# Queuing GpSimd's fetches, gathers, normalising and bias additions behind a slot's probability multiplies

## The chip, the cores and the metric

The kernel is one program on one core of a Trainium2 chip. The metric is the device time of one execution in microseconds; lower is better. Five engines work side by side, each through its own queue of instructions in order: TensorE (PE in the profile, with its weight loads as PEld), VectorE (DVE), ScalarE (ACT), GpSimd (POOL) and SyncE (SP). In this kernel GpSimd does arithmetic and also issues the DMAs that fetch rows by index, so that an issue and an addition stand in one line.

## The reference, cut to what matters

The input is 16 batches of 224 tokens of width 512, and for each batch a context of 750 rows of width 384 with a mask of the keys that count. The layer is a gated cross attention, then a gated feed-forward block whose two weights are rounded to -1, 0 or 1 and whose activations are rounded to 8 bits.

```python
q = layernorm(x) @ W_q                    # 8 heads of 64
k, v = context @ W_k, context @ W_v
sim = where(mask, q k^T / 8, -max)        # per batch and head
out = softmax(sim) v
x = x + tanh(g_xattn) * (out @ W_o + b_o)
h = bitlinear(layernorm(x), w1, b1)       # rmsnorm, 8-bit rows, ternary weights; 512 -> 2048
h = gelu(h)
x = x + tanh(g_ffn) * bitlinear(h, w2, b2)   # 2048 -> 512
```

## The kernel before, in words

**Slots.** The batches are sorted by how many keys their mask keeps, and each is worked on in a "slot" with a fixed room for keys: 192 in slots 0 to 7, 128 in slots 8 to 13, 64 in slots 14 and 15. Only the kept context rows are gathered. Token rows are taken in pairs of 128-row tiles: `x_i` (three buffers) is a pair to be normalised for the queries, and `y_i` (three buffers) the same rows again as the residual for what follows. There are 14 pairs. The gathered context `ctx_s` has two buffers.

**Attention of slot s.** The 8 heads and 224 queries are cut into four units n = 0 to 3. `scores` multiplies queries by keys on TensorE (`sim`, L1106), takes the masked logits and their maximum on DVE (L1120), the exponentials and their sums on ACT (L1130), the reciprocal `rec` of the sums on DVE (L1139), and multiplies the probabilities `p_s_n` by it on GpSimd (L1140). `turn_probs` transposes the probabilities on TensorE into `ptp` (L1163) and, where a slot has more than 128 keys, `ptr` (L1170); DVE or ACT copies them to `pT`, and `weighted` multiplies by the values (`av`, L1188). Units 0 and 1 of a slot are scored at the end of the slot before it, units 2 and 3 in the middle of the slot.

**Work for later slots, in the same loop pass.** For slot s+2: `norm(i)` takes statistics of a pair x_i on DVE and, on GpSimd, `rs_x`, `ls_x` (L1014, L1017), a power (L795) and the normalising itself (L1019, two instructions); `fetch` issues the next x pair (L808, two DMAs), and `gather` the context rows (L908, one or two DMAs). For slot s+1: the context is turned (`ctxp`, L935) and projected (`kp`, L946; `vp`, L962), and the queries are projected (`qp`, L1066). `select` builds the list of kept keys (`ind` on DVE, L846).

**The feed-forward block of pair i.** In slots 0 and 1 its weights are rounded and turned instead (`raw`, `w`, `wp`). From slot 2 on, `residual(i)` fetches y_i (L808, two DMAs) and adds the bias `bo` on GpSimd (L1245, two additions). `project(i, k)` multiplies by W_o on TensorE (`op`, L1252) and DVE adds the result to y (L1255). `normalise(i)` follows on DVE with its scale chain on GpSimd (L1307, L795, L1272 to L1274) and the bias `b2` (L1312). `up` is the first product (`hp`, L1333), `down` the second (`fp`, L1475), whose result DVE adds to y (L1488) and GpSimd stores (L1494). Slot 2 takes pair 0, slot 8 pair 6, slot 9 none, slot 10 pair 7, and slot 15 pair 12; pair 13 is done behind the loop. In a pass the order is `residual`, `up` of the pair before, `project`, `down`; in slots 2 and 10 there is no `up`.

**What sets the order.** In each pass three streams (attention, work for later slots, feed-forward) are merged by written costs; pieces with cost 0.0 come where they fall. A tile scheduler then orders every engine's queue from this program, from its own estimates of time and from when buffers come free; an engine works through its queue strictly in that order. `tc.issue_after(x)` says that what is issued inside it comes behind instruction x. The PSUM results of transposes and projections (`ptp`, `ptr`, `op`, `fp`, `vp`, `ctxp`) share four buffers of one pool, each of which comes free when the engine that reads it is done.

Of the kernel before, what the change touches and what calls it, by code (L numbers as in the profile page):

```python
# [11 lines left out]
ALU = mybir.AluOpType  # L12
# [722 lines left out]
def compact_path(ctx, tc, sh, x, context, out, late_loads, stages):  # L735
# [3 lines left out]
    nc = tc.nc  # L739
    P = 128  # L740
    B, S, D = x.shape
# [11 lines left out]
    NTOK = B * S // P  # L753
# [64 lines left out]
    live = [{} for _ in range(B + 1)]  # L818
# [9 lines left out]
    def home(s):  # L828

        return live[min(s, B - 2)], CAPS[s] if s == B - 1 else 0  # L830
# [162 lines left out]
    def fetch(i):  # L993
        if i:
            xp = pa.tile([P, 2, D], F32, tag="x", name=f"x_{i}", bufs=3)
        else:
            xp = early[:, : 2 * D].rearrange("p (k d) -> p k d", k=2)
        for k in range(2):
            fetch_x(xp[:, k, :], 2 * i + k)
        normed[i] = xp  # L1000

    def norm(i, ks=(0, 1)):

        xp = normed[i]
        name = f"x{i}_{ks[0]}"
        part = slice(ks[0], ks[-1] + 1)
        mv = small(f"mv_{name}", 4).rearrange("p (k n) -> p k n", k=2)
        for k in ks:
            st = small(f"bs_{name}_{k}", 6)
            nc.vector.bn_stats(st, xp[:, k, :])  # L1010
            nc.vector.bn_aggr(mv[:, k, :], st)
            load["v"] += 850
        rstd = small(f"rs_{name}")
        nc.gpsimd.tensor_scalar(rstd[:, part], mv[:, part, 1], 1.0, EPS, ALU.mult, ALU.add)  # L1014
        pow_half(rstd[:, part])
        less = small(f"ls_{name}")
        nc.gpsimd.tensor_scalar(less[:, part], mv[:, part, 0], -1.0, 0.0, ALU.mult, ALU.add)  # L1017
        for k in ks:
            nc.gpsimd.tensor_scalar(  # L1019
                xp[:, k, :], xp[:, k, :], less[:, k : k + 1], rstd[:, k : k + 1], ALU.add, ALU.mult  # L1020
            )
# [57 lines left out]
    def tiles_of(s):  # L1079

        return range(-(-s * S // P), -(-(s + 1) * S // P))

    def norm_pieces(s):
        pieces = []
        for t in tiles_of(s):
            if t % 2 == 0:
                pieces.append((0.0, lambda t=t: norm(t // 2)))
                if t // 2 + 2 < NTOK // 2:
                    pieces.append((0.0, lambda t=t: fetch(t // 2 + 2)))
        return pieces  # L1090


    UNITS = [(q, u) for u in range(2) for q in range(NQ)]
# [1 line left out]
    def scores(s, n):  # L1095
        st = live[s]
        keys, first = home(s)
        cap = CAPS[s]
        q, u = UNITS[n]
        sim = wide([TQ, 2, 2, 256], F32, f"sim_{s}_{n}")  # L1100

        begin = P if cap > P else 0
        for i in range(2):
            p = 2 * u + i
            for j in range(2):
                nc.tensor.matmul(  # L1106
                    sim[:, j, i, :cap],
                    lhsT=st["qT"][j * DH : (j + 1) * DH, p, q * TQ : (q + 1) * TQ],
                    rhs=keys["kT"][j * DH : (j + 1) * DH, p, first + j * begin : first + j * begin + cap],
                    start=True,  # L1110
                    stop=True,
                )
        probs = pa.tile([TQ, 4, 192], F32, tag="p", name=f"p_{s}_{n}", bufs=3)
        total = small(f"sum_{s}_{n}", 4)
        for i in range(2):
            for j in range(2):
                h = 2 * i + j
                nmax = pa.tile([TQ, 1], F32, tag="nm", name=f"nm_{s}_{n}_{h}", bufs=12)

                nc.vector.tensor_tensor_reduce(  # L1120
                    out=probs[:, h, :cap],
                    in0=sim[:, j, i, :cap],
                    in1=keys["mask"][:, first + j * begin : first + j * begin + cap],
                    scale=-(DH**-0.5),
                    scalar=FMAX,
                    op0=ALU.add,
                    op1=ALU.min,
                    accum_out=nmax,
                )
                nc.scalar.activation(  # L1130
                    probs[:, h, :cap],
                    probs[:, h, :cap],
                    AF.Exp,
                    bias=nmax,
                    scale=-1.0,
                    accum_out=total[:TQ, h : h + 1],
                )
        rec = small(f"rec_{s}_{n}", 4)
        nc.vector.reciprocal(rec[:TQ], total[:TQ])  # L1139
        nc.gpsimd.tensor_tensor(  # L1140
            probs[:, :, first : first + cap],
            probs[:, :, :cap],
            rec[:TQ].unsqueeze(2).to_broadcast([TQ, 4, cap]),
            ALU.mult,
        )
        load["v"] += 4 * (150 + 1.05 * cap + 83) + 150
        load["s"] += 4 * (250 + 0.96 * cap + 187)
        st["p", n] = probs
# [63 lines left out]
        for a in range(2):  # L1212
            evict(xoT[:, 2 * a : 2 * a + 2, at : at + S], by[:, a], 2 * S)

    def attention_pieces(s):
        a = 4.0 if CAPS[s] > P else 2.6
        t = 0.8 if CAPS[s] > P else 0.5
        c = 1.4 if CAPS[s] > P else 1.0

        def both(n):  # L1220
            scores(s, n)
            scores(s, n + 1)

        def wait():
            pass

        pieces = [(3.0, wait)]
        pieces += [(t, lambda n=n: turn_probs(s, n)) for n in (0, 1)]
        pieces += [(c, lambda: both(2)), (3.0, wait)]
        pieces += [(t, lambda n=n: turn_probs(s, n)) for n in (2, 3)]  # L1230
        pieces += [(1.0, wait), (a, lambda: weighted(s))]
        return pieces
# [2 lines left out]
    pairs = {}  # L1235
    late = {}

    def residual(i):

        f = pairs[i] = {}  # L1240
        f["y"] = y = late["rows"].tile([P, 2, D], F32, tag="y", name=f"y_{i}", bufs=3)
        for k in range(2):
            fetch_x(y[:, k, :], 2 * i + k)
        for k in range(2):
            nc.gpsimd.tensor_tensor(y[:, k, :], y[:, k, :], sh.bo, ALU.add)  # L1245

    def project(i, k):
        y = pairs[i]["y"]
# [446 lines left out]
    with ExitStack() as behind:  # L1695
        for instruction in latest.values():
            behind.enter_context(tc.issue_after(instruction))
        scores(0, 0)
        scores(0, 1)
        for _, piece in queries[3:] + keys_values[3:]:  # L1700
            piece()
        for c in range(NPC):
            sum_weights(0, c)
        scale_weights(0)
        for _, piece in norm_pieces(1):
            piece()
        select(2)

        held = [sh.wo[0:1, 0, 0:1], sh.wo[0:1, 2, 0:1], sh.wo[P // 2 : P // 2 + 1, 2, 0:1]]
        for dst in held + [sh.bo[0:1, 0:1], sh.b1[0:1, 0:1], sh.b2[0:1, 0:1]]:  # L1710
            nc.scalar.copy(dst, weight_sums[0][0:1, NPC - 1 : NPC])
    late_loads(True)

# [1 line left out]

    projected = raised = lowered = 0
    for s in range(B):
        other = norm_pieces(s + 2) if s + 2 < B else []
        if s + 2 < B:
            other.append((0.0, lambda s=s: gather(s + 2)))  # L1720
        if s + 3 < B:
            other.append((0.0, lambda s=s: select(s + 3)))
        if s + 1 < B:
            other += weave(context_pieces(s + 1), query_pieces(s + 1))
        flow = []
        if s < 2:
            flow = weight_pieces(s)
        else:
            complete = 256 * (projected + 1) <= S * s
            if projected == 0:  # L1730
                nc.gpsimd.tensor_scalar(sh.bo, sh.bo, sh.tgates[:, 0:1], None, ALU.mult)
                nc.gpsimd.tensor_scalar(sh.b2, sh.b2, sh.tgates[:, 1:2], None, ALU.mult)
            if complete:
                flow.append((0.0, lambda i=projected: residual(i)))
            if s == B - 1:
                flow += last_slot(projected)
            elif raised < projected:
                flow += up_pieces(raised)
                raised += 1
            if complete and s < B - 1:  # L1740
                flow += project_pieces(projected)
                projected += 1
                if lowered < raised:
                    flow += down_pieces(lowered)
                    lowered += 1
        merge(attention_pieces(s), other, flow)
        if s == 1:

            late["stage"].close()
            late["rows"] = ctx.enter_context(tc.tile_pool(name="rows", bufs=1))  # L1750
        if s + 1 < B:
            scores(s + 1, 0)
            scores(s + 1, 1)
# [17 lines left out]
        NTOK - 1: [(0, 128, where[2] + 96)],  # L1771
    }
    i = NPAIR - 1
    residual(i)
    with tc.issue_after(late["av"]), tc.issue_after(late["rounded"]):
        for k in range(2):
            for g in range(2):
# [10 lines left out]
    with tc.issue_after(late["rounded"]):  # L1788
        with tc.issue_after(lowered):
            projected = project(i, 0)  # L1790
# [3 lines left out]
    with tc.issue_after(normed):  # L1794
        with tc.issue_after(pairs[i - 1]["turned"]):
            projected = project(i, 1)
# [65 lines left out]
```

## Time and profile before

| | |
|---|---|
| runs | 723.97, 723.9 and 726.18 us; median 723.97 |
| profiled execution | span 726.0 us; of the three runs 726.18 is the one near it |
| busy TensorE, DVE, ACT, GpSimd | 674.0, 493.1, 413.0, 391.5 us |
| mean clock granted to TensorE | 0.986 of full |
| GpSimd's multiplies of probabilities (L1140) | 64 instructions, 78.6 us |

The span runs from the first to the last instruction. In the profile a row of a timeline has its start, its length, engine, line, operation, the tiles written and read with their shapes, and in brackets how long the engine was idle before and for what it waited. A row of TensorE's waits has the waiting instruction, what it waited for, the sum in microseconds, how often, and the longest.

### The profile page before, as it was taken

To read this page: it belongs to the slowest core of one execution; us is meant where nothing else is said; L and a number is where in the kernel's file an instruction comes from. 1 tells how busy PE (TensorE), PEld (TensorE's weight loads), DVE (VectorE), ACT (ScalarE), POOL (GpSimd) and SP (SyncE) were. 2 spreads that over 40 slices of the span, in tenths; PEclk is the share of its full clock that TensorE was granted. 3 is DMA by queue.
4 is the path that set the end of the run, shared out by engine and by line. 5 is a ranking of instruction groups with operands and counts; after the bars stand their busy time and mean duration, and the time that the engine had idled before them with its cause. 6 is when DMAs were issued, how large, how long until landed. Compare 5 with 4: busy or idle time off the path is not lost.

```text
span 726.0 us, 11445 instructions
## 1 busy us (share of the span) xinstructions
PE 674.0 (93%) x3917; PEld 430.3 (59%) x3917; DVE 493.1 (68%) x1296; ACT 413.0 (57%) x974; POOL 391.5 (54%) x545
## 2 busy tenths in 40 slices
PE   4996899999989999999798999999999999999984
PEld 3774686765656555656565566566666556554432
DVE  5495666777477476675575966757859393869993
ACT  2556664377484672674566646837556563656642
POOL 5584478553494444735646656457554535276441
PEclk9998999999999999999999999999999999999998
DMA  7784031022232122213232331312313222142211
GB/s 239 288 277 162 0 84 51 18 60 53 68 85 60 54 59 59 85 29 90 60 45 90 83 78 46 66 44 74 82 46 59 73 54 77 30 99 47 69 33 49
DMA packets 80146, 56.74 MB, mean 78 GB/s; under 512 B 68208, under 2 KB 68352, under 8 KB 79952
## 3 DMA queue, kind: packets, MB, share of 16 engines
q1 hardware_dynamic: 72336, 31.22, 18.1%
q0 software_dynamic: 7744, 24.71, 11.1%
q8 instruction: 33, 0.54, 0.3%
q14 instruction: 33, 0.27, 0.1%
HBM read 32.06 MB, written 7.34 MB: 54 GB/s over the span
## 4 chain that ended last, share of the span: by engine, by line
PE 56%; DVE 13%; issue 13%; POOL 10%; ACT 4%; DMA 2%; POOLq 0%; DVEq 0%
PE qp L1066 10%; PE op L1252 9%; PE hp L1333 8%; PE fp L1475 6%; PE kp L946 4%; PE sim L1106 4%; PE vp L962 4%; PE ptp L1163 3%; PE av L1188 2%; DVE a L1369 2%; POOL p L1140 2%; POOL out_dram L1494 1%; DVE hq L1372 1%; PE xnp L1045 1%; POOL y L1312 1%
## 5 line engine op out<-in xcount | busy, mean ns | idle before, releaser
L1140 POOL TENSOR_TENSOR p<-p,rec 112x768 f32<-112x768 f32 (+2 forms) x64 | 78.6, 1230 | 74.9 <-DVE rec L1139 28.8
L1130 ACT ACTIVATE p<-p,nm 112x192 f32<-112x192 f32 (+2 forms) x256 | 104.7, 412 | 9.9 <-DVE nm L1120 6.8
L1066 PE MATMUL qp<-xnT,wq_sb 128*128 128x224 f32 x512 | 105.3, 359 | 0.6 <-issue 0.6
L1252 PE MATMUL op<-wo_sb,xoT 128*128 128x512 f32 x224 | 104.0, 599 | 0.0
L1475 PE MATMUL fp<-w2T,hqT 128*128 128x512 fp8e4 x448 | 101.4, 379 | 2.4 <-ACT hqT L1355 1.3
L1333 PE MATMUL hp<-w1T,xqT 128*128 128x512 fp8e4 x416 | 99.7, 384 | 3.0 <-DVE nm L1120 1.3
L1066 PEld LDWEIGHTS qp<-xnT,wq_sb 128*128 128x128 f32 x512 | 97.1, 194 | 6.4 <-issue 4.1
L1341 DVE SCALAR_TENSOR_TENSOR h<-hp,c,b_bc 128x1024 f32<-128x1024 f32 x52 | 66.5, 1280 | 43.8 <-PE hp L1333 43.5
L1120 DVE CUSTOM_DVE_ANT_0 p<-sim,mask 112x192 f32<-112x192 f32 (+2 forms) x224 | 56.0, 303 | 31.9 <-PE sim L1106 31.5
L1475 PEld LDWEIGHTS <-hqT 128*128 128x128 bf16 x448 | 42.7, 98 | 56.3 <-issue 5.3
L1369 DVE TENSOR_REDUCE a<-h 128x1 f32<-128x2048 f32 x26 | 59.3, 2281 | 20.3 <-ACT h L1366 20.1
L1333 PEld LDWEIGHTS <-xqT 128*128 128x128 bf16 x416 | 40.0, 98 | 47.6 <-issue 8.9
L1252 PEld LDWEIGHTS op<-wo_sb,xoT 128*128 128x128 f32 x224 | 40.6, 190 | 38.3 <-issue 35.9
L1488 DVE SCALAR_TENSOR_TENSOR y<-fp,c,y 128x512 f32<-128x512 f32 x28 | 20.8, 745 | 62.1 <-PE fp L1475 59.3
L1494 POOL DMA_INDIRECT out_dram<-y,token x24 | 27.6, 1148 | 58.0 <-DVE y L1488 53.6
L946 PE MATMUL kp<-ctxT,wk_sb 128*128 128x192 f32 (+1 forms) x360 | 57.8, 308 | 0.0
L1382 ACT ACTIVATE h<-h 128x2048 f32<-128x2048 f32 x25 | 47.7, 1909 | 17.1 <-DVE hq L1372 11.8
L1312 POOL TENSOR_TENSOR y<-y,b_bc 128x512 f32<-128x512 f32 x28 | 37.0, 1322 | 37.2 <-DVE fx L1292 36.9
L781 ACT COPY pT<-ptp 128x448 f32<-128x448 f32 (+1 forms) x62 | 32.2, 535 | 42.2 <-PE ptp L1163 41.4
L946 PEld LDWEIGHTS kp<-ctxT,wk_sb 128*128 128x128 f32 x360 | 52.4, 193 | 5.5 <-issue 3.8
L1106 PE MATMUL sim<-kT,qT 64*112 64x192 f32 (+2 forms) x512 | 51.5, 314 | 1.8 <-issue 0.9
L781 ACT COPY qT<-qp 128x448 f32<-128x448 f32 x29 | 15.4, 532 | 65.9 <-PE qp L1066 60.3
(199 smaller groups left out, 1249.3 us busy)
## 6 DMA issues: line engine op xcount, KB each, us to landing
raw<-in_L_ffn_w_dram SPq DMA_DIRECT2D x16, 512.0 KB
wq_sb<-in_L_xattn_W_q_dram SPq DMA_DIRECT2D x1, 1024.0 KB
b_bc<-in_L_ffn_b_dram SPq DMA_DIRECT2D x1, 1024.0 KB
wk_sb<-in_L_xattn_W_k_dram SPq DMA_DIRECT2D x1, 768.0 KB
wv_sb<-in_L_xattn_W_v_dram SPq DMA_DIRECT2D x1, 768.0 KB
wo_sb<-in_L_xattn_W_o_dram SPq DMA_DIRECT2D x1, 512.0 KB
wo_sb<-in_L_xattn_W_o_dram SPq DMA_DIRECT2D x2, 256.0 KB
out_dram<-y SPq DMA_DIRECT2D x2, 256.0 KB
```

What stands on the lines that cost most here:

```text
L946: nc.tensor.matmul(pk[:, p - p0, :], lhsT=sh.wk[:, c, p * P : (p + 1) * P], rhs=st["ctxT"][:, c, :cap], start=(c == 0), stop=(c == NC - 1),)
L1066: nc.tensor.matmul(pq[:, i, :], lhsT=sh.wq[:, d, (p + i) * P : (p + i + 1) * P], rhs=st["xnT"][:, d, :], start=(d == 0), stop=(d == ND - 1),)
L1106: nc.tensor.matmul(sim[:, j, i, :cap], lhsT=st["qT"][j * DH : (j + 1) * DH, p, q * TQ : (q + 1) * TQ], rhs=keys["kT"][j * DH : (j + 1) * D ...
L1120: nc.vector.tensor_tensor_reduce(out=probs[:, h, :cap], in0=sim[:, j, i, :cap], in1=keys["mask"][:, first + j * begin : first + j * begin ...
L1130: nc.scalar.activation(probs[:, h, :cap], probs[:, h, :cap], AF.Exp, bias=nmax, scale=-1.0, accum_out=total[:TQ, h : h + 1],)
L1140: nc.gpsimd.tensor_tensor(probs[:, :, first : first + cap], probs[:, :, :cap], rec[:TQ].unsqueeze(2).to_broadcast([TQ, 4, cap]), ALU.mult,)
L1252: last = nc.tensor.matmul(po, lhsT=xoT[:, d, at : at + P], rhs=sh.wo[:, d, :], start=(d == 0), stop=(d == ND - 1))
L1333: last = nc.tensor.matmul(ph[:, n, :], lhsT=f["xqT"][:, k * ND + d, :], rhs=w1T[:, d, at : at + NB], start=(d == 0), stop=(d == ND - 1),)
L1341: nc.vector.scalar_tensor_tensor(h[:, cols], ph.rearrange("t i n -> t (i n)"), f["c1", k], sh.b1[:, cols], ALU.mult, ALU.add)
L1369: nc.vector.tensor_reduce(amax[:, k : k + 1], h, AX.X, ALU.max, apply_absolute_value=True)
L1382: nc.scalar.activation(f["h", k], f["h", k], AF.Square, accum_out=ss[:, k : k + 1])
L1475: last = nc.tensor.matmul(po, lhsT=f["hqT", k][:, n, :], rhs=w2T[:, n, :], start=(n == 0), stop=(n == NF - 1))
```

## The change

The pieces of work for later slots no longer fall where GpSimd's queue takes them. `scores` keeps the multiply of each unit as `scaled[s, n]`. From slot 2 on, the normalising, the fetch of x and the gather of a pass are issued behind the multiply of unit 1 of the slot; in slots 0 and 1 the fetch and the gather are issued behind unit 3, and the normalising stays as it was. In `residual` the two additions of `bo` go behind the multiply of unit 1 (for pair 13, behind unit 3 of slot 15); the fetches of y stay ahead. The fetch of an x pair is a piece of its own, emitted where the buffer comes free, behind the odd tile of a pair: three pairs ahead, where it was two pairs ahead at the normalising; `fetch(3)` moves to the prologue. No operation is added or taken away: all engines have as many instructions as before.

```diff
--- before.py
+++ after.py
@@ -1081,13 +1081,20 @@
         return range(-(-s * S // P), -(-(s + 1) * S // P))
 
     def norm_pieces(s):
-        pieces = []
-        for t in tiles_of(s):
-            if t % 2 == 0:
-                pieces.append((0.0, lambda t=t: norm(t // 2)))
-                if t // 2 + 2 < NTOK // 2:
-                    pieces.append((0.0, lambda t=t: fetch(t // 2 + 2)))
-        return pieces
+        return [(0.0, lambda t=t: norm(t // 2)) for t in tiles_of(s) if t % 2 == 0]
+
+    def fetch_pieces(s):
+
+        ahead = [t // 2 + 3 for t in tiles_of(s) if t % 2]
+        return [(0.0, lambda i=i: fetch(i)) for i in ahead if i < NTOK // 2]
+
+    def held(s, n, pieces):
+
+        def run(piece):
+            with tc.issue_after(live[s]["scaled", n]):
+                piece()
+
+        return [(c, lambda piece=piece: run(piece)) for c, piece in pieces]
 
 
     UNITS = [(q, u) for u in range(2) for q in range(NQ)]
@@ -1137,12 +1144,12 @@
                 )
         rec = small(f"rec_{s}_{n}", 4)
         nc.vector.reciprocal(rec[:TQ], total[:TQ])
-        nc.gpsimd.tensor_tensor(
+        st["scaled", n] = nc.gpsimd.tensor_tensor(
             probs[:, :, first : first + cap],
             probs[:, :, :cap],
             rec[:TQ].unsqueeze(2).to_broadcast([TQ, 4, cap]),
             ALU.mult,
-        )
+        ).ins
         load["v"] += 4 * (150 + 1.05 * cap + 83) + 150
         load["s"] += 4 * (250 + 0.96 * cap + 187)
         st["p", n] = probs
@@ -1212,7 +1219,7 @@
         for a in range(2):
             evict(xoT[:, 2 * a : 2 * a + 2, at : at + S], by[:, a], 2 * S)
 
-    def attention_pieces(s):
+    def attention_pieces(s, behind=()):
         a = 4.0 if CAPS[s] > P else 2.6
         t = 0.8 if CAPS[s] > P else 0.5
         c = 1.4 if CAPS[s] > P else 1.0
@@ -1226,7 +1233,7 @@
 
         pieces = [(3.0, wait)]
         pieces += [(t, lambda n=n: turn_probs(s, n)) for n in (0, 1)]
-        pieces += [(c, lambda: both(2)), (3.0, wait)]
+        pieces += [(c, lambda: both(2))] + list(behind) + [(3.0, wait)]
         pieces += [(t, lambda n=n: turn_probs(s, n)) for n in (2, 3)]
         pieces += [(1.0, wait), (a, lambda: weighted(s))]
         return pieces
@@ -1235,14 +1242,15 @@
     pairs = {}
     late = {}
 
-    def residual(i):
+    def residual(i, scaled):
 
         f = pairs[i] = {}
         f["y"] = y = late["rows"].tile([P, 2, D], F32, tag="y", name=f"y_{i}", bufs=3)
         for k in range(2):
             fetch_x(y[:, k, :], 2 * i + k)
-        for k in range(2):
-            nc.gpsimd.tensor_tensor(y[:, k, :], y[:, k, :], sh.bo, ALU.add)
+        with tc.issue_after(scaled):
+            for k in range(2):
+                nc.gpsimd.tensor_tensor(y[:, k, :], y[:, k, :], sh.bo, ALU.add)
 
     def project(i, k):
         y = pairs[i]["y"]
@@ -1704,10 +1712,11 @@
         scale_weights(0)
         for _, piece in norm_pieces(1):
             piece()
+        fetch(3)
         select(2)
 
-        held = [sh.wo[0:1, 0, 0:1], sh.wo[0:1, 2, 0:1], sh.wo[P // 2 : P // 2 + 1, 2, 0:1]]
-        for dst in held + [sh.bo[0:1, 0:1], sh.b1[0:1, 0:1], sh.b2[0:1, 0:1]]:
+        opened = [sh.wo[0:1, 0, 0:1], sh.wo[0:1, 2, 0:1], sh.wo[P // 2 : P // 2 + 1, 2, 0:1]]
+        for dst in opened + [sh.bo[0:1, 0:1], sh.b1[0:1, 0:1], sh.b2[0:1, 0:1]]:
             nc.scalar.copy(dst, weight_sums[0][0:1, NPC - 1 : NPC])
     late_loads(True)
 
@@ -1715,9 +1724,13 @@
 
     projected = raised = lowered = 0
     for s in range(B):
-        other = norm_pieces(s + 2) if s + 2 < B else []
+        other, loads = [], []
         if s + 2 < B:
-            other.append((0.0, lambda s=s: gather(s + 2)))
+            other = norm_pieces(s + 2)
+            loads = fetch_pieces(s + 1) + [(0.0, lambda s=s: gather(s + 2))]
+        if s > 1:
+
+            other, loads = held(s, 1, other + loads), []
         if s + 3 < B:
             other.append((0.0, lambda s=s: select(s + 3)))
         if s + 1 < B:
@@ -1731,7 +1744,7 @@
                 nc.gpsimd.tensor_scalar(sh.bo, sh.bo, sh.tgates[:, 0:1], None, ALU.mult)
                 nc.gpsimd.tensor_scalar(sh.b2, sh.b2, sh.tgates[:, 1:2], None, ALU.mult)
             if complete:
-                flow.append((0.0, lambda i=projected: residual(i)))
+                flow.append((0.0, lambda i=projected, s=s: residual(i, live[s]["scaled", 1])))
             if s == B - 1:
                 flow += last_slot(projected)
             elif raised < projected:
@@ -1743,7 +1756,7 @@
                 if lowered < raised:
                     flow += down_pieces(lowered)
                     lowered += 1
-        merge(attention_pieces(s), other, flow)
+        merge(attention_pieces(s, held(s, 3, loads)), other, flow)
         if s == 1:
 
             late["stage"].close()
@@ -1771,7 +1784,7 @@
         NTOK - 1: [(0, 128, where[2] + 96)],
     }
     i = NPAIR - 1
-    residual(i)
+    residual(i, live[B - 1]["scaled", 3])
     with tc.issue_after(late["av"]), tc.issue_after(late["rounded"]):
         for k in range(2):
             for g in range(2):
```

## The prediction

> **What bounds the kernel now.** I read the page first, then TensorE's waits, then the timelines at the longest of them.
>
> ```profile
> span 726.0 us, 11445 instructions
> ...
> PE 674.0 (93%) x3917; PEld 430.3 (59%) x3917; DVE 493.1 (68%) x1296; ACT 413.0 (57%) x974; POOL 391.5 (54%) x545
> PE   4996899999989999999798999999999999999984
> PE ptp L1163 <- POOL p L1140: 16.9, 10, 5.6
> PE pk L108 <- DVE diag L106: 4.2, 1, 4.2
> ```
>
> TensorE is busy for 674.0 of 726.0 us: the bound. No operation is added or removed, so a gain can only come from its 52 us of idle time and from matmuls run at a lowered clock. The first row of its waits is 16.9 us in ten waits of the transposes `ptp` for GpSimd's multiply of probabilities, the work that the change moves other things behind. All ten, by place: 5.55 us at 62.23 (slot 0); 1.07, 1.39, 1.47, 3.65 and 1.17 us at 206.37, 255.42, 303.38, 350.37 and 398.73 (slots 4 to 8); 0.35, 0.43 and 1.02 us (slot 9); 0.77 us at 662.60 (slot 15). The longest two, GpSimd first:
>
> ```profile
> 53.71 2.42 POOL L908 DMA_INDIRECT ctx<-in_ctx_dram,keys  x1 [0.17 <-issue]
> 56.43 1.69 POOL L808 DMA_INDIRECT x<-in_x_dram,token  x1 [0.30 <-PE qp L1066]
> 58.42 1.00 POOL L808 DMA_INDIRECT x<-in_x_dram,token  x1 [0.30 <-issue]
> 59.72 0.95 POOL L908 DMA_INDIRECT ctx<-in_ctx_dram,keys  x1 [0.31 <-issue]
> 60.70 2.90 POOL L1140 TENSOR_TENSOR p<-p,rec 112x768 f32<-112x768 f32 x2
> 62.23 1.01 PE L1163 MATMUL ptp<-ident,p 112*128 112x112 f32 x4 [5.55 <-POOL p L1140]
> ...
> 347.62 1.28 POOL L1245 TENSOR_TENSOR y<-y,bo_bc 128x512 f32<-128x512 f32 x1
> 348.85 1.47 POOL L1140 TENSOR_TENSOR p<-p,rec 112x768 f32<-112x768 f32 x1
> 350.37 0.60 PE L1163 MATMUL ptp<-ident,p 112*128 112x112 f32 x4 [3.65 <-POOL p L1140]
> ```
>
> In slot 0 the reciprocals that the two multiplies need end at 54.16 and 56.75, yet GpSimd issues four DMAs first. In slot 7 a `y` fetch and two additions of `bo` stand ahead. These are queue waits, not data waits. The clock afterwards (columns: window, width, busy PE, PEld, DVE, ACT and POOL, PEclk, DMA share, GB/s):
>
> ```profile
> 60.00:64.00 4.00, 1.77 (x10) 1.23 (x12) 0.95 (x1) 2.44 (x4) 3.57 (x3) 0.62 0.85 336
> 64.00:68.00 4.00, 4.00 (x26) 2.65 (x23) 0.74 (x2) 1.36 (x2) 0.00 (x0) 0.53 0.00 0
> 88.00:92.00 4.00, 3.91 (x21) 3.57 (x22) 4.00 (x8) 1.88 (x4) 3.83 (x3) 0.57 0.00 0
> 348.00:352.00 4.00, 1.63 (x9) 1.04 (x10) 0.00 (x0) 2.58 (x4) 3.54 (x4) 0.89 0.18 53
> 352.00:356.00 4.00, 4.00 (x15) 1.72 (x14) 1.43 (x2) 0.63 (x2) 3.69 (x6) 0.69 0.51 131
> ```
>
> Busy time times the missing clock gives what the cold matmuls lost: 1.77 x 0.38 + 4.00 x 0.47 = 2.6 us in slot 0; 1.63 x 0.11 + 4.00 x 0.31 = 1.4 us in slot 7; 3.91 x 0.43 = 1.7 us at 88, behind 3.3 us of waits for DVE.
>
> **The change, part by part.** TensorE's order differs in one matmul (a `sim` of slot 2, one place ahead), ACT's and SP's not at all. On DVE, slot 2's `pT` copy moves ahead of a statistic of y_0, and slot 10's addition to y_7 behind `rec_10_2`. GpSimd's order changes everywhere.
>
> *Slot 0, fetch and gather behind unit 3.* Ahead of `p_0_2` four DMA issues disappear: 2.42 + 1.69 + 1.00 + 0.95 us and gaps of 0.3, 53.71 to 60.70. `p_0_2` then starts when its reciprocal (54.16) and the norm of x_2 (53.54) are done, and ends by 57.5 at the slowest; `p_0_3` by 60. Both were 62.2 and 63.6. TensorE was free from 56.67. It doesn't gain it all: ACT works without a break until 61.9 (sums and casts of weights) and evicts `pT` only then, where before it idled 1.36 us ahead of that copy at 63.27. Following the order, the transposes, half of `av`, the `wp` turns and the scores of slot 1 fit in 57.5 to 62, and `vp`, whose buffer waits for the second `pT` copy, starts near 62.9 where it was 69.72: 6.8 us. If ACT's copy alone sets the pace it is 1.4; the wait with its cold clock is 5.55 + 2.6 = 8.2. I take 6.0, near the upper rows because the matmuls between are work for which TensorE no longer waits. The moved issues (x_4 twice, ctx_2 twice, about 1.3 us each) end near 65; their first reader, `ctxp` of slot 2, ran at 81.6, so the cover is 9 us after this shift. Gain 6.0 (1.4 to 8.2).
>
> *Slot 1.* No wait there was GpSimd's. ctx_3 and x_5 land near 100 instead; `ctxp` of slot 3 ran at 116. Nothing, with 9 us of cover.
>
> *Slots 4 to 8, norm, fetch, gather and `bo` behind unit 1.* The five waits make 1.07 + 1.39 + 1.47 + 3.65 + 1.17 = 8.75 us, with 1.4 of clock in slot 7: 10.15. I checked slot 7, where most stood ahead: the out store (338.35) and both y fetches (341.46, 342.84) remain in front, and `p_7_0`, whose reciprocal ended at 344.15, can end at 345.6; TensorE wants it at 346.72. In all five slots the reciprocal ended 4.3 to 4.7 us before the multiply began. Who waits now: `y<-op` (L1255) for `bo`. In slot 3 the same run of norm and gather took 154.58 to 161.32, so `bo` of y_1's first half ends at 164.5; the addition was at 169.03. In slot 4: 211 against 218.13. Margins of 4 to 7 us in all slots where `up` comes ahead of `project`: nothing lost. Other limits can surface (TensorE waits 0.94 us for DVE at 214.49), so 6 to 11.
>
> *Slot 9.* 0.43 and 1.02 us stay: GpSimd itself was waiting for DVE's reciprocal. 0.35 stays too, behind a y fetch.
>
> *Slot 2, the new wait.* Here nothing is raised yet, so `project` comes first and its addition is early. The lines of before:
>
> ```profile
> 108.44 2.50 POOL L1245 TENSOR_TENSOR y<-y,bo_bc 128x512 f32<-128x512 f32 x2
> 121.90 1.47 POOL L1140 TENSOR_TENSOR p<-p,rec 112x768 f32<-112x768 f32 x1 [0.86 <-DVE mv_x L1011]
> 121.79 0.71 DVE L1255 SCALAR_TENSOR_TENSOR y<-op,tgates,y 128x512 f32<-128x512 f32 x1
> 124.57 0.55 PE L1163 MATMUL ptp<-ident,p 112*128 112x112 f32 x4
> ```
>
> `bo` for y_0 goes from 108.44 to behind `p_2_1` (reciprocal at 121.73), two small operations, a ctx issue, the power, another ctx issue and the norm of x_4: 6.74 us by slot 3's sequence, plus 1.27 = 8.0, so 129.7. DVE waits in order, adds until 130.4, and `ptp_2_1`, whose PSUM buffer that addition frees, starts there and not at 124.57: 5.9 us. It may be 2 us less: `ind` on DVE took 3.31 us for five at 118.34 beside GpSimd and 1.16 for six at 69.07. I take 5.0, between 3.5 and 6. Behind the DVE instruction stand `rec_2_2`'s work and the `pT` copies; ACT and TensorE wait for them within the same stretch.
>
> The clock: rows show 1.4 to 1.7 lost after stops of 3.3 to 3.65 us. The Trainium skill, "TensorE: Matmul & The Clock Gate", Part 1, says that the array falls to half clock after an idle window of about 3.4 us and takes as long of work to return. It speaks against this part: a 5 us stop is a whole window, and 3.4 us at half clock lose 1.7. Without clock loss the slot would cost 5.0, by the rule 6.7, by the rows 6.4 to 6.7, up to slot 0's 2.6. I take 6.6 (3.5 to 8.6).
>
> *Slot 10.* Also no `up` first. `fp_6_0` (472.89) now needs the buffer freed by the addition to y_7, whose `bo` follows `p_10_0`, `p_10_1`, rs, ls, a ctx issue and the power: near 473.8, addition until 474.65: 1.8 us (0 to 4).
>
> *Tail.* 2 x 1.27 = 2.6 us of `bo` for y_13 now stand behind `p_15_3` (661.93), ahead of the scale chain of pair 12. It would end 2.6 later than 666.8; DVE, its reader, reaches it at 672.07. Nothing (0 to 2.6).
>
> *Sum:* -6.0 - 10.15 + 6.6 + 1.8 = -7.8 us on the profiled 726.0 (its run is the 726.18; the other two are near 723.9, 2.2 below, and I carry the difference over): 723.97 - 7.8 = 716.2.
>
> **The rivals.**
> *A, the waits move on.* TensorE starts earlier and stops for ACT or DVE instead: slot 0 gives 1.4, slots 4 to 8 give 8, slots 2 and 10 cost 8.4: -1, about 723. For it: ACT's unbroken chain to 61.9, and DVE at 68%. Against: in slots 4 to 8 the reciprocals were ready over 4 us ahead, and the copies behind `ptp` have not stood in TensorE's longest waits.
>
> *B, slower: `bo` behind the norm.* GpSimd runs slowly beside DVE: the norm took 3.95 us at 87.45 (usually 1.5) and one pass over `bo_bc` 5.03 at 43.77. With 2.4 more for the norm and 1.3 for `bo`, slot 2's chain is 11.7, the stop 9.5 and the clock 2.6; slot 10 costs 3. That is 15.1 against 1.4 + 10.15 = 11.6 where slot 0 also fails: +3.5, 727.5. It decides from the point where slots 2 and 10 together pass what slots 0 and 4 to 8 give. Margins of 4 us in slot 3 would then vanish too, and add a stop per slot. Against: no such slow norm is seen after 92.
>
> *C, nothing.* GpSimd's order would not matter if the waits were data waits; ruled out for seven of ten by the reciprocals' times.
>
> **How the numbers follow.** My forecast has 0.62 and 716; A 0.18, ending on both sides of zero; B 0.18; C 0.02. About 0.3%, 2.2 us, is what a measurement of this kernel can tell from no change. Faster: 0.62 and half of A, 0.71; same: 0.08; slower: B and a rest of A, 0.21. All upper gains with the lowest costs give -16, all the reverse +8; the range leaves out the outer tenth at each side: 709.5 to 726.
>
> **What would show it.** Right: the row of `ptp` waits falls from 16.9 to 3 or 4 us; `ptp` of slot 0 near 58 and `vp` near 63; a new TensorE wait of 4 to 6 us in slot 2 on DVE's `y<-op`, DVE itself waiting for L1253 of the new kernel, with a clock below 0.75 behind it; the row of slots 4 to 8 gone. Wrong: `vp` after 67 (A); a norm of over 3 us in slot 2, or waits on `y<-op` in slots 3 to 8 (B); a tail longer by over 1 us.

## The result: slower by 1.5%

The changed kernel takes 736.14 us (median of four runs, 734.92 to 736.75) against 724.65 us before: ratio 1.0145, 95% interval 1.0124 to 1.0166. Its profiled execution is the run of 736.75 us, span 735.0 us. The forecast was 716.2 us.

The page of the changed kernel and TensorE's waits (waiting instruction, what it waited for, sum in us, times, longest):

```profile
PE 680.9 (93%) x3917; PEld 436.4 (59%) x3917; DVE 501.8 (68%) x1296; ACT 412.6 (56%) x974; POOL 391.3 (53%) x545
...
PE hp L1341 <- DVE nm L1127: 8.8, 4, 3.1
PE ptp L1170 <- DVE y L1263: 4.6, 1, 4.6
PE pk L108 <- DVE diag L106: 4.1, 1, 4.1
PE ptp L1170 <- POOL p L1147: 3.1, 5, 1.0
```

The row that the change was about fell as forecast: `ptp` behind GpSimd's multiply from 16.9 to 3.1 us. The stop in slot 2 is there (4.57 us on DVE's `y<-op`). What was not forecast is the new first row: the first product of the feed-forward block waits 8.8 us for DVE. And DVE, with the same 1296 instructions, is busy 8.7 us longer (493.1 to 501.8). Some DVE instruction has become slower. The timelines of slot 7, where the longest of these stops is, show which (DVE, GpSimd and TensorE of the changed kernel):

```profile
358.60 1.43 DVE L1380 TENSOR_SCALAR hq<-h,k 128x2048 int16<-128x2048 f32 x1
360.49 3.56 DVE L1382 CAST hq<-hq 128x2048 bf16<-128x2048 int16 x1
363.96 0.34 DVE L1127 CUSTOM_DVE_ANT_0 p<-sim,mask 112x192 f32<-112x192 f32 x1
360.99 2.49 POOL L1253 TENSOR_TENSOR y<-y,bo_bc 128x512 f32<-128x512 f32 x2
364.93 1.89 PE L1341 MATMUL hp<-w1T,xqT 128*128 128x512 fp8e4 x8 [3.06 <-DVE nm L1127]
```

The same cast in the kernel before took 0.69 us, and the first of the two additions of this pair stood 15 us ahead of it:

```profile
345.16 1.28 POOL L1245 TENSOR_TENSOR y<-y,bo_bc 128x512 f32<-128x512 f32 x1 [1.31 <-DMA y<-in_x_dram,token]
360.43 0.69 DVE L1374 CAST hq<-hq 128x2048 bf16<-128x2048 int16 x1
```

The two `bo` additions, which in that kernel ran at 345.16 and 347.62, now run from 360.99 to 363.48, and the cast that begins at 360.49 ends half a microsecond behind them. Behind it in DVE's queue stand the maxima of the next scores; the `hp` matmul needs the PSUM buffer that they free. Going through all 26 pairs of scaling (L1380) and cast (L1382) of the changed kernel gives the same picture in five slots (in slot 5 the scaling meets only the end of one addition and takes 1.72 us, without a stop), and the tail has it on another instruction:

| place | DVE instruction, us | without company | GpSimd beside it | TensorE's stop |
|---|---|---|---|---|
| slot 3, 168.01 | cast 3.00 | 0.69 | `bo` 167.95 to 170.45 | 1.58 |
| slot 4, 214.99 | scaling 4.14 | 1.28 | a context issue, then `bo` | 2.13 |
| slot 6, 309.72 | scaling 3.46 | 1.28 | `bo` | 1.98 |
| slot 7, 360.49 | cast 3.56 | 0.69 | a context issue, then `bo` | 3.06 |
| slot 11, 506.79 | scaling 3.23 | 1.28 | `bo` | 1.92, a `sim` for `h<-hp` |
| tail, 668.28 | `fx` 3.09 | 0.68 | `bo` of y_13, 668.58 to 671.08 | 2.19, for the transposing DMA that follows |

Each is longer by 2.0 to 2.9 us, about the time of the pair (2.5); in slots 4 and 7, the longest two, GpSimd was also issuing a DMA of context rows when the DVE instruction began.

### The profile page after: what moved, and what is told of

Its sections match the earlier page's. It is cut to its first block, busy times and chain, and to the rows that moved or that the text cites. A ratio compares the mean times of both kernels' runs of the same rounds, so it can differ in the third digit from the quotient of the medians.

```text
span 735.0 us, 11472 instructions
## 1 busy us (share of the span) xinstructions
PE 680.9 (93%) x3917; PEld 436.4 (59%) x3917; DVE 501.8 (68%) x1296; ACT 412.6 (56%) x974; POOL 391.3 (53%) x545
## 4 chain that ended last, share of the span: by engine, by line
PE 71%; DVE 15%; DMA 3%; ACT 3%; POOL 2%; issue 2%; DVEq 0%; POOLq 0%; ACTq 0%
PE hp L1341 11%; PE op L1260 11%; PE fp L1483 11%; PE qp L1066 10%; PE kp L946 5%; PE vp L962 5%; PE sim L1113 5%; PE av L1195 3%; PE ptp L1170 2%; DVE a L1377 2%; DVE hq L1380 2%; DMA raw<-in_L_ffn_w_dram 2%; DVE h L1349 2%; PE xnp L1045 2%; PE ctxp L935 1%
## 5 line engine op out<-in xcount | busy, mean ns | idle before, releaser
L1147 POOL TENSOR_TENSOR p<-p,rec 112x768 f32<-112x768 f32 (+2 forms) x64 | 82.2, 1284 | 104.5 <-DVE rec L1146 52.5
L1260 PE MATMUL op<-wo_sb,xoT 128*128 128x512 f32 x224 | 106.1, 610 | 0.0
L946 PE MATMUL kp<-ctxT,wk_sb 128*128 128x192 f32 (+1 forms) x360 | 60.1, 316 | 0.0
L946 PEld LDWEIGHTS kp<-ctxT,wk_sb 128*128 128x128 f32 x360 | 54.8, 199 | 5.8 <-issue 3.4
L1113 PEld LDWEIGHTS sim<-kT,qT 64*112 64x112 f32 x512 | 38.4, 176 | 23.9 <-issue 12.5
```

The source lines that it names most:

```text
L946: nc.tensor.matmul(pk[:, p - p0, :], lhsT=sh.wk[:, c, p * P : (p + 1) * P], rhs=st["ctxT"][:, c, :cap], start=(c == 0), stop=(c == NC - 1),)
L1113: nc.tensor.matmul(sim[:, j, i, :cap], lhsT=st["qT"][j * DH : (j + 1) * DH, p, q * TQ : (q + 1) * TQ], rhs=keys["kT"][j * DH : (j + 1) * D ...
L1147: st["scaled", n] = nc.gpsimd.tensor_tensor(probs[:, :, first : first + cap], probs[:, :, :cap], rec[:TQ].unsqueeze(2).to_broadcast([TQ, 4 ...
L1260: last = nc.tensor.matmul(po, lhsT=xoT[:, d, at : at + P], rhs=sh.wo[:, d, :], start=(d == 0), stop=(d == ND - 1))
```

## The experiments

Three theories were set against each other. T: the loss is this meeting of the two `bo` additions with DVE's scaling, cast and `fx`, and beside it the wait of slot 2 and slot 10. W: only the late `bo` in slots 2 and 10. N: the held norm, fetches and gathers. The diffs show the lines that matter, without line numbers; "changed" is the changed kernel.

**1. bo_free: no hold on `bo`.**

```diff
 def residual(i, scaled):
-        with tc.issue_after(scaled):
+        with ExitStack():
             for k in range(2):
                 nc.gpsimd.tensor_tensor(y[:, k, :], y[:, k, :], sh.bo, ALU.add)
```

> The changed kernel with the hold on the bo additions taken away everywhere; the norm, the fetches and the gathers stay held. Theory T (held behind the norm, the two bo additions fall beside DVE's scaling and cast of hq in slots 3, 4, 6, 7 and 11 and beside fx in the tail, and stretch those DVE instructions; in slots 2 and 10 they also make DVE and TensorE wait): of 736 us the slot 2, slot 10 and tail losses (6.2 + 1.8 + 3) and most of the stops of slots 3, 4, 6, 7, 11 (10.7 us and about 1.4 of clock) go, while bo stands ahead of p again in slots 4 to 8 and takes back 2 to 5 us: 715 to 720. Rival W (only the late bo matters, through y<-op of slots 2 and 10): 727 to 729. Rival N (the held norm, fetches and gathers are what costs): 734 to 737.

717.17 us, ratio to before 0.9893 (0.9869 to 0.9917). W and N fall: the hold on `bo` costs 18 to 19 us where the norm is held too, and everything else in the change together is worth over 1%. The waits for `p` came back only in slot 7 (2.47 us) and, new, in slot 2 (1.04).

**2. bo_thin: the additions stay where they are, on an eighth of the columns.**

```diff
-                nc.gpsimd.tensor_tensor(y[:, k, :], y[:, k, :], sh.bo, ALU.add)
+                nc.gpsimd.tensor_tensor(y[:, k, :64], y[:, k, :64], sh.bo[:, :64], ALU.add)
```

> The changed kernel with each bo addition on 64 of its 512 columns; the other columns stay without bo. The place in GpSimd's queue is that of the changed kernel. Theory T: hq scaling and cast return to 1.3 and 0.7 us, fx in the tail to 0.7; TensorE's waits in slots 3, 4, 6, 7 and 11 (1.58, 2.13, 1.98, 3.06, 1.92 us) fall below 0.5 each, and slot 2's 4.57 to about 3.4; 719 to 723. Rival W: only slot 2 and slot 10 get shorter, by the 1 us that the first addition is shorter: 733 to 735. Rival N: 734 to 737.

719.49 us, ratio 0.9918 (0.9889 to 0.9947). DVE's cast of slot 3, then TensorE's first wait and the largest one left on DVE's maxima:

```profile
167.57 0.83 DVE L1382 CAST hq<-hq 128x2048 bf16<-128x2048 int16 x1
...
PE ptp L1170 <- DVE y L1263: 4.1, 1, 4.1
...
354.38 1.89 PE L1341 MATMUL hp<-w1T,xqT 128*128 128x512 fp8e4 x8 [0.47 <-DVE nm L1127]
```

The queue's order hardly differs from the changed kernel's (one `sim` on TensorE, two swaps on DVE), so it is the length of the addition, not its place in the order, that sets the stops of slots 3 to 11. Slot 2's wait lost less than expected (4.14 where 3.4 was written). Where a thin addition still meets DVE, it can be GpSimd that waits, as in slot 6:

```profile
305.12 1.59 POOL L1253 TENSOR_TENSOR y<-y,bo_bc 128x64 f32<-128x64 f32 x2
305.25 1.29 DVE L1380 TENSOR_SCALAR hq<-h,k 128x2048 int16<-128x2048 f32 x1
```

The scaling keeps its time, and the pair takes 1.59 us; at 257.25 it took 0.61.

**3. bo_free_2_10_end: no hold on `bo` in slots 2 and 10 and for pair 13.**

```diff
-        with tc.issue_after(scaled):
+        with ExitStack() if i in (0, 7, NPAIR - 1) else tc.issue_after(scaled):
```

> The changed kernel with the bo additions of pairs 0, 7 and 13 (slots 2 and 10 and the tail) not held, all others held. Theory T: the waits of slot 2 (4.57 us and cold clock), slot 10 (1.56) and the tail (DVE's fx of 3.09 us, 3 us at the end) go, those of slots 3, 4, 6, 7 and 11 stay: 724 to 727. Rival W: all of the loss is in slots 2 and 10, so the time falls under the kernel before, to 715 to 718. Rival N: 734 to 737.

724.5 us, ratio 0.9984 (0.9971 to 0.9996). As T had it: the waits of slots 2 and 10 are gone, and those of slots 3, 4, 6, 7 and 11 stand at 1.58, 2.09, 1.95, 3.07 and 1.92 us, the same to 0.04.

**4. bo_ahead_of_norm: as 3, with `bo` still behind unit 1 but ahead of the norm.** The residual is issued before the pieces for later slots, and these are held behind its second addition.

```diff
+        if complete:
+            residual(projected, live[s]["scaled", 1])
 ...
         if s > 1:
-            other, loads = held(s, 1, other + loads), []
+            added = pairs[projected]["added"] if complete and projected not in (0, 7) else None
+            other, loads = held(s, 1, other + loads, added), []
```

> The last kernel, with the bo additions of the other slots still behind the multiply of unit 1 but ahead of the norm, the fetch and the gather, which are held behind them. They end some 4 us before DVE scales hq. Theory T: no hq scaling or cast beside a bo addition, TensorE's waits of slots 3, 4, 6, 7, 11 below 0.5 us each, no waits of ptp for p in slots 4 to 8: 711 to 716. Rival M (a held bo addition stretches some DVE instruction wherever it falls): 722 to 727, as without this move.

712.7 us, ratio 0.9822 (0.9803 to 0.9842): the fastest of all, and 11.8 us under experiment 3, from which it differs by this order; TensorE, DVE and ACT run the same instructions in the same order in both. Slot 7 on GpSimd and DVE:

```profile
336.89 1.47 POOL L1147 TENSOR_TENSOR p<-p,rec 112x768 f32<-112x768 f32 x1 [0.73 <-DVE mv_x L1011]
338.31 2.52 POOL L1253 TENSOR_TENSOR y<-y,bo_bc 128x512 f32<-128x512 f32 x2
339.46 1.28 DVE L1349 SCALAR_TENSOR_TENSOR h<-hp,c,b_bc 128x1024 f32<-128x1024 f32 x1 [2.58 <-PE hp L1341]
343.35 1.29 DVE L1380 TENSOR_SCALAR hq<-h,k 128x2048 int16<-128x2048 f32 x1
345.23 0.98 DVE L1382 CAST hq<-hq 128x2048 bf16<-128x2048 int16 x1
```

The additions now meet `h<-hp` on DVE, which reads PSUM, and that one keeps its 1.28 us. They end 2.5 us before the scaling starts. In slot 8 they meet the row maximum `a<-h`, which reads the same 2048 columns of SBUF as the scaling, and it keeps its time too:

```profile
383.38 2.51 POOL L1253 TENSOR_TENSOR y<-y,bo_bc 128x512 f32<-128x512 f32 x2
383.87 2.28 DVE L1377 TENSOR_REDUCE a<-h 128x1 f32<-128x2048 f32 x1
```

Rival M falls: it is not any DVE instruction that suffers. One meeting is left, in slot 15, where the freed addition to y_13 stretches a scaling to 2.23 us.

**5. bo_only: the kernel before with nothing but the hold on `bo`.**

```diff
-        for k in range(2):
-            nc.gpsimd.tensor_tensor(y[:, k, :], y[:, k, :], sh.bo, ALU.add)
+        with tc.issue_after(scaled):
+            for k in range(2):
+                nc.gpsimd.tensor_tensor(y[:, k, :], y[:, k, :], sh.bo, ALU.add)
```

> The kernel before with the hold on bo alone; norm, fetches and gathers as before. The scheduler then puts the two additions directly behind the multiply of unit 1, ahead of the norm and the gather. Theory T (it is the place behind the norm, fetch and gather, beside hq, that costs, not the hold): hq scaling and cast stay at 1.3 to 1.9 and 0.7 us, the waits of slots 4 to 8 (10 us with the clock) go, slot 2, slot 10 and the tail cost some 5.5, slot 0 stays: 718 to 722. Rival H (a bo addition behind unit 1 costs wherever it stands): 730 to 738.

717.11 us, ratio 0.9889 (0.9855 to 0.9923). So the same hold that costs 18 to 19 us behind a held norm gains 1.1% alone. In slot 2 `ptp` waits 0.35 us for `y<-op` where the changed kernel waits 4.57, and no cast is over 1.2 us; two scalings (slots 7 and 8) still meet a `bo` addition and take 2.30 and 1.73. The tail is as in the changed kernel:

```profile
647.62 3.18 DVE L1293 TENSOR_SCALAR fx<-y,mv_y 128x512 f32<-128x512 f32 x1
648.01 2.51 POOL L1246 TENSOR_TENSOR y<-y,bo_bc 128x512 f32<-128x512 f32 x2
```

TensorE waits 2.12 us there, so the hold of pair 13 costs time in this kernel as well.

**6. slots_0_1_only: no hold from slot 2 on.**

```diff
-            other, loads = held(s, 1, other + loads), []
+            other, loads = other + loads, []
 ...
-        with tc.issue_after(scaled):
+        with ExitStack():
```

> The changed kernel with all holds from slot 2 on taken away, those on bo included: what stays are the fetches and gathers of slots 0 and 1 behind unit 3 and the new place of the fetch pieces. In the kernels so far the second scores of slot 1 came 2.1 to 4.6 us earlier than before, so this part is worth 2 to 5 us: 720 to 723, with the five waits of ptp for p in slots 4 to 8 (8.75 us) still there. If slot 0 is worth the 6 us that were forecast: 717 to 719. If what was gained is the hold of the norm in slots 4 to 8 alone: 724 to 726.

731.61 us, ratio 1.0069 (1.0047 to 1.0091): a miss, slower instead of faster. The waits of slots 4 to 8 are there as expected. Two places lose time. First, `p_2_0` stands behind the free `bo` additions of three pairs, which begin at 110.06 here and at 105.27 in the second profile of before (experiment 8), because the held x and ctx issues of slot 1 now stand ahead of them: 1.55 us at 122.75, and a lowered clock with it (0.87 from 120 to 124 us, 0.70 from 124 to 128). Second, two stops of 0.76 and 1.05 us in the weight turns at 110, put down to nothing that the profile shows; experiment 7 has the same two (0.71 and 1.05), the others have none. What causes them stays open. From experiment 1 this kernel differs only by the hold on the norm, the fetches and the gathers from slot 2 on: the two unexplained stops apart, it is that hold that gains there, and the part in slots 0 and 1 gains nothing here.

**7. bo_one_input: another instruction in the place of `bo`.**

```diff
-                nc.gpsimd.tensor_tensor(y[:, k, :], y[:, k, :], sh.bo, ALU.add)
+                nc.gpsimd.tensor_scalar(y[:, k, :], y[:, k, :], sh.tgates[:, 0:1], None, ALU.add)
```

> The changed kernel with each bo addition replaced by an addition of one number per row (a tensor_scalar with one tensor as input; bo itself is left out), on all 512 columns, in the same order on all engines. It takes about 0.76 us as the norm's two do, where the two-input addition took 1.25. If only a GpSimd instruction with two tensors as input holds DVE up: hq 1.3 and cast 0.7 us, waits of slots 3, 4, 6, 7, 11 below 0.5 us, 719 to 723. If any GpSimd arithmetic does: hq or the cast longer by the 1.5 us of the pair in each of these slots, 726 to 730.

725.5 us, ratio 0.9983 (0.9971 to 0.9995), between the two cases. DVE and GpSimd in slot 3, and a pair on GpSimd in slot 2 and in slot 6:

```profile
170.26 1.20 DVE L1382 CAST hq<-hq 128x2048 bf16<-128x2048 int16 x1
170.22 3.25 POOL L1253 TENSOR_SCALAR y<-y,tgates 128x512 f32<-128x512 f32 x2
...
126.59 3.12 POOL L1253 TENSOR_SCALAR y<-y,tgates 128x512 f32<-128x512 f32 x2
307.83 4.44 POOL L1253 TENSOR_SCALAR y<-y,tgates 128x512 f32<-128x512 f32 x2
```

The cast loses 0.5 us, not 2.3, and the scalings of slots 4 to 6 lose 0.4 to 0.5. The five stops are 0.63 us or less. But the new instruction is not the short one that was expected: the pair of slot 2, beside no scaling or cast, takes 3.12 us, where 1.5 was expected and the pair of `bo` takes 2.5. So the 3.25 us of slot 3 is nearly its own length, while in slot 6 (4.44) GpSimd waits as well as DVE. The 6 us over bo_thin are for the most part the longer pair ahead of its readers in slot 2 (a wait of 4.90), slot 10 (1.94) and the tail (1.65), and the two unexplained stops. The run changes two things at once, the number of tensor inputs and the pace, and it does not show that the second input is what holds DVE. Against that: in the kernel before, a cast of 3.26 us at 210.90 ran beside one norm pair (one tensor input) and one `bo` addition, and in bo_free the scaling of slot 6 took 1.82 us beside a norm pair that began at 299.96, 0.04 us ahead of it.

**8. before_again: a second profile of the kernel before.**

> The kernel before, unchanged, for a second profile: TensorE's clock at 40 to 52 us was 1.00 in the first one and 0.5 to 0.6 for 7 to 13 us in all five kernels with the change's slots 0 and 1. If the change causes it, the clock here stays at 1.00 up to the wait at 62 us; if it depends on the run, it falls below 0.8 in one of the windows 40 to 52.

726.18 us in its one run, span 724.1. Its slot 0, waits and windows (window, width, busy PE, PEld, DVE, ACT, POOL, PEclk, DMA share, GB/s):

```profile
60.44 0.60 PE L1163 MATMUL ptp<-ident,p 112*128 112x112 f32 x4 [0.80 <-POOL p L1140]
...
PE ptp L1163 <- POOL p L1140: 12.4, 11, 3.7
...
44.00:48.00 4.00, 2.90 (x21) 2.48 (x20) 3.74 (x8) 1.85 (x4) 3.83 (x4) 0.61 1.01 343
48.00:52.00 4.00, 4.00 (x17) 3.91 (x16) 2.91 (x11) 0.81 (x3) 3.88 (x4) 0.53 0.95 303
```

The 5.55 us wait of slot 0 is 0.80 us here, and `ptp` starts earlier, at 60.44 for 62.23. In this execution the clock was low from 44 to 52 us, so TensorE came to `ptp` when `p` was nearly ready (at 59.64, where it stood free from 56.67 in the first; `p` itself was ready some 1.8 us earlier); in the first it kept full clock, arrived early, stood 5.55 us and had a low clock afterwards. The waits of slots 4 to 8 are the same in both profiles to 0.2 us. Of the ten profiles on record only the first one of before has full clock from 40 to 52 us. The low clock there is in the changed kernel and in bo_only too (0.50 from 44 to 48 in both), so it does not need the change; what brings it stays open.

## Why the prediction was wrong, point by point

The starts of the same ACT instructions (ACT's order is the same in both) give what each stretch of the changed kernel costs against the second profile of before:

| stretch | forecast, us | measured, us |
|---|---|---|
| slots 0 and 1 | -6.0 | +0.8 |
| slot 2 | +6.6 | +6.5 |
| slots 3 to 8 | -10.15 | -3.3 |
| slot 9 | 0 | -0.8 |
| slot 10 | +1.8 | +1.7 |
| slot 11 | 0 | +2.9 |
| slots 12 to 15 and tail | 0 | +2.8 |
| sum | -7.8 | +10.6 |

The spans differ by 735.0 - 724.1 = 10.9. Against the first profile, on which the forecast was made, slots 0 and 1 are at -2.0 and the sum is +9.0; the other stretches differ from the table by 0.8 at most.

**Slots 4 to 8: the waits went, and the cover was another engine's.** The step that failed is "Margins of 4 to 7 us in all slots where `up` comes ahead of `project`: nothing lost". It asked only who reads what `bo` writes. That reader did get it in time, 3.0 to 9.1 us ahead in slots 3 to 8. What was not asked is what else runs on DVE while GpSimd adds: the move (in slot 7 from 345.16 to 360.99) puts the pair beside the scaling and the cast of `hq` in slots 3, 4, 6, 7 and 11. The stops there make 1.58 + 2.13 + 1.98 + 3.06 + 1.92 = 10.7 us, with low clock behind some of them (0.65 at 316 to 320, 0.67 at 512 to 516; none behind the longest, at 364 to 368). The first four, 8.75 us, cancel the five waits for `p`, which make 8.76 us in the second profile of before. Experiments 2 and 4 show it by size and by place. Rival B came near ("GpSimd runs slowly beside DVE") and took the wrong one of the two as the loser: in these slots GpSimd keeps its 2.5 us and DVE waits. The first profile had rows for that: the 3.26 us cast at 210.90, the 2.33 us scaling at 305.84, and the `ind` rows that the prediction itself used in slot 2, there as a gain and nowhere as a cost. The Trainium skill, "GPSIMD Engine Reference", section 1, says that GpSimd's SBUF interfaces are shared with VectorE, with contention where the DVE instruction runs in a two-port mode or has two SBUF inputs; "VectorE: DVE Perf Modes", "Side-by-side: where the cycles go for N=2048 bf16", gives 693 and 1224 ns for 2048 elements in its modes of four and two elements a cycle and 2293 in the plain one, and the rows are 0.65 to 0.69 for the cast, 1.27 to 1.29 for the scaling and 2.28 for the maximum over the same width. By these paces the cast and the scaling would be the two-port instructions and the maximum not, and the runs agree: the first two are stretched beside `bo`, and the maximum keeps 2.28 us (experiment 4).

**Slot 0: the term came from one execution.** "5.55 + 2.6 = 8.2", of which 6.0 was taken, failed on its first number. The second profile of before has 0.80 us in that place, and slots 0 and 1 of the changed kernel, with the wait at 0.53, are at +0.8. Part of that is clock: busy time times the missing clock from 40 to 52 us is 4.00 x 0.50 + 2.97 x 0.50 + 4.00 x 0.50 = 5.5 us in the changed kernel, and 2.90 x 0.39 + 4.00 x 0.47 = 3.0 in the second profile of before. The first profile was also of a slow execution: in every run of before that is on record with both, the time is about 2.1 us above the span, so that its span of 726.0 belongs to some 728 us (an estimate) and not to the run of 726.18, which the prediction took for it; in the second profile 726.18 us has a span of 724.1. The low end that the prediction gave (1.4, ACT sets the pace) was the nearer: after `ptp` the changed kernel waits 0.60 for a cast and 0.80 for a `pT` copy, both on ACT.

**Slot 2 and slot 10: right in mechanism and size.** DVE stood still for GpSimd 8.05 us in slot 2, as worked out:

```profile
125.28 2.48 POOL L1253 TENSOR_TENSOR y<-y,bo_bc 128x512 f32<-128x512 f32 x2
126.56 0.75 DVE L1263 SCALAR_TENSOR_TENSOR y<-op,tgates,y 128x512 f32<-128x512 f32 x1 [8.05 <-POOL y L1253]
127.37 0.78 PE L1170 MATMUL ptp<-ident,p 112*128 112x112 f32 x4 [4.57 <-DVE y L1263]
```

4.57 us for the stop (5.0 taken); most of the rest of 6.5 is low clock behind it (4.00 x 0.39 = 1.6 us at 128 to 132). That the clock falls after a stop of this length, which the rule of the clock gate was cited for, is seen here. The length of a stop alone does not tell, though: the clock was also low behind the stops of 1.98 and 1.92 us, shorter than the window of the rule. In slot 10 the stop is 1.56 us for 1.8.

**Tail: the term of 0 was 2.4 to 2.8.** The prediction followed GpSimd's chain, 2.6 us late, to a reader that would not notice. The addition did its harm before, beside `fx`, and the clock was low behind the stop (0.65 at 676 to 680):

```profile
668.28 3.09 DVE L1300 TENSOR_SCALAR fx<-y,mv_y 128x512 f32<-128x512 f32 x1
668.58 2.50 POOL L1253 TENSOR_TENSOR y<-y,bo_bc 128x512 f32<-128x512 f32 x2
676.98 7.26 PE L1341 MATMUL hp<-w1T,xqT 128*128 128x512 fp8e4 x25 [2.19 <-DMA xqT<-xq]
```

**Rivals and range.** A (small net) and C did not happen. B has the right sign; its place, slots 2 and 10 beyond their forecast, is not where the loss was. What the prediction held against it, no slow norm after 92, was not quite so: a norm pair at 504.03 of the first profile took 3.04 us. The range ended at 726.0 because a cost in slots 3 to 11 and in the tail was taken as nothing or as 2.6 at most. It was also too narrow for the prediction's own chances: B had 0.18 and lay at 727.5, beyond an end that was to leave out one tenth. And 736.1 lies beyond all terms at their worst, 724 + 8 = 732, so a term was missing and not only mis-sized.

The two holds each gain alone and lose together: 724 to 726 us before, 717.1 with `bo` held alone, 717.2 with norm, fetch and gather held (and slots 0 and 1), 736.1 with all of it, 712.7 with `bo` ahead of the norm and free in slots 2 and 10 and for pair 13.

## What to carry to other kernels

An instruction that is moved on GpSimd has to be checked at its new place against what DVE runs in those microseconds, not only against its readers: beside DVE's scaling or cast of a wide tile in SBUF, two two-input additions of 2.5 us together cost DVE 2 to 3 us and TensorE up to 3.1, while a row maximum over the same tile and an instruction that reads PSUM lost nothing. If a stall stands in one profile only, take a second execution's profile before it becomes a term of the sum. And of two pieces that are held behind the same instruction, the order between them can be worth more than the hold.

## What the runs showed that was not expected

- DVE's cast of 128x2048 took 0.69 us alone and 3.00 to 3.56 us beside two GpSimd additions of two tensors; scaling 1.28 alone, 3.23 to 4.14 beside them; `h<-hp` out of PSUM kept 1.28, and the row maximum over 2048 columns of SBUF kept 2.28.
- It is not always DVE that waits: beside a scaling that kept 1.29 us, a pair of thin additions took 1.59 instead of 0.61, and with one tensor input the pair of slot 6 took 4.44 instead of 3.12. What decides who waits stays open.
- Two executions of one kernel had the clock low at different places (44 to 52 us, or 60 to 68 us) and a wait of 0.80 or 5.55 us with it, and ended 1.9 us apart in span (724.1 and 726.0).
